# The last pass of a two-layer convolution kernel: channels in chunks of 32 on the partitions, 32x32 transposes on VectorE, layer norm over four partition blocks

## The chip, the cores and the metric

The kernel runs on one core of one Trainium2 chip. A core has TensorE (PE; its weight loads are listed as PEld), VectorE (DVE), ScalarE (ACT), GpSimd (POOL) and SyncE (SP), which here only issues DMAs; 16 DMA engines serve all queues. Tiles lie in SBUF with 128 partitions; TensorE writes PSUM, which has eight banks of 512 float32 per partition. The metric is the device time of one execution in microseconds (us). All data are float32.

## The reference

The input `x` is 8 images of 96 x 96 pixels with 192 channels. Two layers follow, each `x = x + layer(group_norm(x))`. Cut to its shape:

```python
# layer 0
proj  = gn(x) @ W_in + b_in                    # 192 -> 384 channels
local = depthwise_conv3x3(proj)
mixed = 0.25 * (four one-sided moving averages of local) + local
x     = x + (layer_norm(mixed) * ln_g + ln_b) @ W_out + b_out

# layer 1
y = depthwise_conv7x7(gn(x), dw_kernel) + dw_bias
mu  = mean(y, axis=-1); var = mean((y - mu)**2, axis=-1)     # over the 192 channels
y = (y - mu) * rsqrt(var + 1e-6) * ln_gamma + ln_beta
y = gelu(y @ w0 + b0)                          # 192 -> 768
y = y @ w1 + b1                                # 768 -> 192
x = x + y * gamma
```

## The kernel before

The program has five stages, one after the other in one instruction stream for each engine, with the order written out by hand (`tc.manual_schedule`). Each engine works through its own instructions in order; semaphores tie the engines together. The first two stages (to about 1808 us) are the projection, the 3x3 convolution and the moving averages of layer 0; they are not touched.

The third stage (to about 2645 us) has 192 units `u`: it loads `mt` and `xr`, multiplies by `wc` (L989), normalises, adds and stores `X1_d`, the input of layer 1. At its start `load_weights` (L728) issues on ScalarE's queue all loads of the weights of the last pass: `w0w` (w0, rows on partitions in three column blocks), `aff` (the layer norm's gamma and beta, one value per partition), `w1g`, biases. Near its end, at `u == n_u - 20`, it loads the first data of the depthwise convolution: `load_band(0)` and three `load_raw(0, t)`.

The fourth stage is the 7x7 depthwise convolution. It works on 32 items `n`, each 12 channels of one half of the batch. `load_raw(n, t)` (L774) brings a third `t` of the input; one half goes through SP's queue, the other through GpSimd's. `scale_steps(n)` (L804) are 24 VectorE scalings `raw` to `xin` (L820) and one copy of `band` (L824). `conv_d(n, c)` (L1126) is 24 matmuls (L1141) into two PSUM banks and two ScalarE copies to `yo`; `store_d(n)` writes `Y_d`. `N1` = 19 items run here. `raw` has three buffers in each of two pools, one of which (`early`) stays for the whole rest of the program.

The fifth stage, the last pass, begins at about 3002 us. It has 72 units `u`, two for each of 36 blocks `n`. A unit is eight image columns by 128 rows. For each block, `load_y(n)` (L1179) reads the convolution's result with four DMAs into `y`, with image rows on the partitions and 192 channels by 16 columns along them; `load_r(n)` reads the residual and `bias_r(n)` (L1200) adds the bias on GpSimd. For each unit:

- `stats_e` (L1204): for each of eight columns a mean and variance over 192 channels (L1209, L1210), then `rsqrt_eps`: an addition on VectorE (L28) and a power on GpSimd (L29).
- `norm_e` (L1215): eight subtract-and-multiply operations (L1219) from `y` to `yn`.
- `turn_in(u, k)` for k = 0, 1, 2 (L1228): four TensorE transposes each (L1236) into the one PSUM bank of `ps_t`, and a VectorE copy of 512 elements to `yT` (L1239), which also turns the order of the rows round. Now channels are on the partitions: block 0 holds channels 0 to 127 of even columns, block 2 channels 64 to 191 of odd columns, and block 1 the remaining 64 of both.
- `first_layer` (L1244): matmuls L1254 over 128 rows and L1264 over 64 rows into PSUM banks `hp`, then Gelu on ScalarE (L1273) into `g`.
- `second_layer(u, k)` for k = 0 to 3 (L1277): matmuls L1284 into one bank, on VectorE the sum with the residual (L1295) to `xo`, and a GpSimd-issued store of the output (L1303).

In iteration `u` of the loop (L1374) the first layer of `u`, the turning of `u + 1`, the statistics and normalisation of `u + 2` and the second layer of `u - 1` are interleaved. In the first half the first layer is split into three parts and only the banks of `ps_h` (five) are used; the remaining 13 items of the convolution are spread over it by `slot()`, five slots per unit from `u` = 2 on, nine slots per item (three of scalings, six of `conv_d`, which uses the two banks of `ps_y`). In the second half the first layer has two parts and takes its banks from both pools in turn. Before the loop stand `prepare(0)` (run beside the last item of stage four), `load_y(0)`, `load_y(1)`, `turn_in(0, k)`, `prepare(1)` and `load_y(2)`. `load_y(m)` is issued at the end of a unit, once `norm_e` has read the buffer that it fills.

## Time and profile before

| | |
|---|---|
| median of three runs | 5611.91 us (5606.21 to 5626.06) |
| the profiled execution: its own time, its span | 5613.02 us, 5611.2 us |
| mean granted TensorE clock | 0.981 |
| busy: PE, DVE, ACT, POOL | 5384.6, 3068.6, 2241.1, 2099.1 us |
| PEld | 3433.2 us |
| L1236, transposes on TensorE | 864, busy 141.2 us, 285 ns each |
| L1239, their copies on VectorE | 216, 689 ns each |
| L1209, L1210, statistics | 576 each, 460 and 182 ns |
| L1219, normalisation | 576, 445 ns |
| L1295, residual sum | 288, 800 ns |
| L1200, bias on GpSimd | 36, 5440 ns |
| DMA moved | 996.64 MB |

A group is named by line, engine, operation, what it writes and what it reads. Busy time is the union of a group's instructions, so that overlapping matmuls are not counted twice; the mean is of one instruction. Idle time before a group names what ended the wait. A float32 matmul appears as two instructions where it multiplies (24 for L1254 per unit), a transpose as one. Of the span, the last pass is the part after about 3002 us.

### The profile page before, as it was taken

The page shows a single profiled execution, that of the slowest core. Times are in us where ns is not written, and L with a number is a line of the kernel's source. Part 1 is how long each engine was busy: PE and PEld are TensorE (multiplying, and loading weights), DVE is VectorE, ACT ScalarE, POOL GpSimd, SP SyncE. Part 2 cuts the span into 40 slices and gives each one's busy share as a digit, 9 for nine tenths or more (in the row PEclk, how much of TensorE's full clock was granted, in tenths as well). Part 3 has the DMA queues.
Part 4 walks back from the last instruction along what each step waited for, and adds up shares of the span by engine and source line. Part 5 has one row for each costly group of instructions (what it writes and reads, how often), then busy time and mean ns, then how long its engine had stood idle before and what let it go on. Part 6 is the DMA issues. An engine that isn't in the chain of part 4 may idle for free.

```text
span 5611.2 us, 106882 instructions
## 1 busy us (share of the span) xinstructions
PE 5384.6 (96%) x43070; PEld 3433.2 (61%) x43070; DVE 3068.6 (55%) x6331; ACT 2241.1 (40%) x5306; POOL 2099.1 (37%) x2086
## 2 busy tenths in 40 slices
PE   5999989999999999998777999999999999999999
PEld 3666643333333899997344666666666676767677
DVE  5555549999999355555454454444444343333332
ACT  2444447777776566565332222222222222222221
POOL 1111128888888455554222222222222222222221
PEclk9999989999999999999888999999999999999999
DMA  7999869999998899999997456555332223332321
GB/s 199 284 286 278 236 195 245 245 245 243 244 245 214 250 283 283 280 289 275 266 275 173 107 119 133 122 130 116 96 75 69 70 68 78 71 71 68 75 63 40
DMA packets 698886, 996.64 MB, mean 178 GB/s; under 512 B 237415, under 2 KB 579992, under 8 KB 696344
## 3 DMA queue, kind: packets, MB, share of 16 engines
q1 hardware_dynamic: 602200, 622.03, 44.8%
q0 software_dynamic: 90064, 365.17, 20.8%
q8 instruction: 340, 5.57, 0.4%
q10 hardware_dynamic: 6128, 2.61, 0.2%
q14 instruction: 154, 1.26, 0.1%
HBM read 585.22 MB, written 419.95 MB: 179 GB/s over the span
## 4 chain that ended last, share of the span: by engine, by line
PE 45%; DMA 4%; issue 2%; DVE 1%; POOL 0%; SPq 0%; ACT 0%; POOLq 0%; DVEq 0%; ACTq 0%
PE hp L1284 19%; PE hp L1254 13%; PE hp L1264 7%; PE hp L1141 4%; PE pt L1236 2%; DMA raw<-X 2%; DMA band<-Z_d 2%; DVE xin L820 1%; DMA r<-X 0%; DVE band L824 0%; DMA Y<-yo 0%; ACT xin L818 0%; POOL out_dram L1303 0%; SPq L789 0%; POOL r L1200 0%
## 5 line engine op out<-in xcount | busy, mean ns | idle before, releaser
L1284 PE MATMUL hp<-w1g,g 128*128 128x192 f32 x6912 | 1168.6, 328 | 3.4 <-DVE xo L1295 3.2
L1273 ACT ACTIVATE g<-hp,b0g 128x512 f32<-128x512 f32 x864 | 519.0, 691 | 1627.6 <-PE hp L1264 1627.6
L1284 PEld LDWEIGHTS hp<-w1g,g 128*128 128x128 f32 x6912 | 1123.1, 191 | 40.3 <-issue 19.3
L1303 POOL DMA_DIRECT2D out_dram<-xo x288 | 211.6, 735 | 1617.7 <-DVE xo L1295 1575.9
L1254 PE MATMUL hp<-yT,w0w 128*128 128x512 f32 x1728 | 778.4, 597 | 0.0
L989 PE MATMUL po<-wc,mt 128*128 128x193 f32 x3456 | 685.1, 334 | 1.8 <-DVE x1c L1006 1.8
L1239 DVE COPY yT<-pt 128x512 f32<-128x512 f32 x216 | 148.9, 689 | 926.9 <-PE pt L1236 926.8
L600 PE MATMUL pl<-pin,band 34*32 34x380 f32 (+1 forms) x13824 | 628.3, 489 | 18.7 <-DMA pin<-P_d 18.7
L674 POOL TENSOR_TENSOR mo<-mo,z 128x768 f32<-128x768 f32 x286 | 598.6, 2093 | 2.9
L989 PEld LDWEIGHTS po<-wc,mt 128*128 128x128 f32 x3456 | 554.9, 191 | 32.5 <-ACT mean L991 30.3
L1254 PEld LDWEIGHTS hp<-yT,w0w 128*128 128x128 f32 x1728 | 319.7, 190 | 356.8 <-issue 347.2
L633 DVE TENSOR_TENSOR_SCAN z<-decay,loc 128x768 f32<-128x768 f32 x288 | 505.7, 1756 | 41.4 <-ACT loc L609 12.2
L1295 DVE TENSOR_TENSOR xo<-hp,r 128x384 f32<-128x384 f32 x288 | 230.5, 800 | 524.6 <-PE hp L1284 524.6
L1141 PE MATMUL hp<-xin,band 63*64 63x372 f32 (+1 forms) x4608 | 428.5, 511 | 77.0 <-DMA band<-Z_d 38.2
L642 DVE TENSOR_TENSOR_SCAN z<-decay,z 128x768 f32<-128x768 f32 x288 | 498.2, 1730 | 0.1
L600 PEld LDWEIGHTS pl<-pin,band 34*32 34x32 f32 x13824 | 232.2, 107 | 396.5 <-issue 394.6
L621 PE MATMUL pa<-loc,mix 128*32 128x384 f32 x3456 | 431.6, 493 | 0.0
L1151 ACT ACTIVATE yo<-hp,dwb 128x384 f32<-128x384 f32 x384 | 201.6, 577 | 567.6 <-PE hp L1141 440.7
L624 PE MATMUL pa<-last,down 96*32 96x384 f32 x1152 | 426.6, 493 | 0.9 <-ACT mo L625 0.9
L1264 PE MATMUL hp<-yT,w0w 64*128 64x512 f32 x1728 | 419.6, 611 | 0.0
L382 PE MATMUL pm<-xT,win 128*128 128x384 f32 x1152 | 395.1, 493 | 8.1 <-DVE po L406 8.1
L609 ACT COPY loc<-pl 128x384 f32<-128x384 f32 x576 | 248.1, 483 | 311.0 <-PE pl L600 311.0
(143 smaller groups left out, 6636.3 us busy)
## 6 DMA issues: line engine op xcount, KB each, us to landing
P_d<-po POOLq DMA_DIRECT2D x96, 1152.0 KB, 9.8
pin<-P_d SPq DMA_DIRECT2D x192, 576.0 KB
mt<-M SPq DMA_DIRECT2D x192, 384.0 KB
xq<-in_x_dram SPq DMA_DIRECT2D x96, 576.0 KB
xr<-in_x_dram SPq DMA_DIRECT2D x192, 288.0 KB
X<-x1c SPq DMA_DIRECT2D x144, 384.0 KB
y<-Y SPq DMA_DIRECT2D x144, 384.0 KB
r<-X SPq DMA_DIRECT2D x36, 1536.0 KB
```

What stands on the lines that cost most here:

```text
L600: nc.tensor.matmul(pls[g][at * RB : (at + 1) * RB, :, lo:hi], band[rows, c, kh, :], pin[rows, c, :, NJ - 1 - j, lo + kh - 1 : hi + kh - 1] ...
L621: nc.tensor.matmul(pa[at], mix[:, i, at], loc[:, q], start=True, stop=True)
L624: nc.tensor.matmul(pa[at], down[:, to], last[:, q], start=True, stop=True)
L633: nc.vector.tensor_tensor_scan(zf, decay_f, loc.rearrange("p q n -> p (q n)"), 0.0, ALU.mult, ALU.add)
L642: nc.vector.tensor_tensor_scan(zr, decay_f, zr, 0.0, ALU.mult, ALU.add)
L674: eng.tensor_tensor(m, m, z, ALU.add)
L989: nc.tensor.matmul(po, lhs[m], wc[:, m], start=(m == 0), stop=(m == NC - 1))
L1141: nc.tensor.matmul(pys[g][k * 64 : (k + 1) * 64, :, lo:hi], band[rows, k * GS + c, d * ZS : d * ZS + 64], xin[rows, :, :, k * GS + c, lo + ...
L1254: nc.tensor.matmul(hps[m, q], w0w[:, 2 * q, m * 128 : (m + 1) * 128], yT[:, 2 * q], start=True, stop=False,)
L1264: nc.tensor.matmul(hps[m, q], w0w[p, 1, m * 128 : (m + 1) * 128], yT[p, 1], start=False, stop=True,)
L1273: nc.scalar.activation(g[:, m, q], hps[m, q], AF.Gelu, bias=b0g[:, m : m + 1], scale=1.0)
L1284: nc.tensor.matmul(po[:, q], g[:, m, q, k * 128 : (k + 1) * 128], w1g[:, m], start=(m == 0), stop=(m == NE - 1),)
```

## The change

`y` is read in another layout. The 192 channels are cut into six chunks of 32. Four chunks lie on the four partition blocks of 32 in tile `ya`; chunks 4 and 5 lie in tile `yb`, each twice: once for the first four columns of a unit and once, shifted by `HV` = 4 columns, for the last four. Within a partition block the 32 partitions are the image rows. The convolution stores groups of six channels, so a chunk is five whole groups and two channels of a later group; the rows of `w0` and of the layer norm's gamma and beta are loaded in the same permuted order. `load_y` becomes 40 DMAs.

A 32x32 transpose of each block on VectorE then puts 32 channels on each block's partitions. TensorE's transposes, their PSUM bank and the copies from PSUM are gone, and `ps_h` has six banks. As the channels of one pixel now lie on several partition blocks, the layer norm becomes six steps, given out over the unit: `sums` (over the 32 channels of each block), `mean` (gather the blocks' sums by short copies onto 32 partitions, add them, copy the mean back to four blocks), `center` (subtract; Square on ScalarE), `squares` (add), `powers` (gather again, power on GpSimd over 32 partitions by 32 columns), `scale` (copy to four blocks, multiply).

A second-layer step now takes columns `v` and `v + 4` in place of `v` and `v + 1`. `load_y(n + 2)` is issued in the first unit of block `n`, after the turning of the block's second unit. `raw` now has two buffers in `early` and four in the other pool; the third `t = 2` is loaded after the first scalings of its own item, and parts of the loads move to earlier slots. `load_weights` returns 54 loads that are issued one per unit of the third stage from `u` = 8.

The diff, cut to its core:

```diff
-    w0w = cp.tile([128, 3, EXP], F32, name="w0w")
+    w0w = cp.tile([128, 2, EXP], F32, name="w0w")
...
     def load_raw(n, t):
         hf, i = todo[n]
-        pool = d_pools[0 if n == 0 or n >= N1 else (n + 1) % 2]
-        raw = pool.tile([128, NH, NV, GC, WQ], F32, tag="raw", name="raw", bufs=NT)
+        own = 0 < n < N1 and (n % 2 == 0 or t == NT - 1)
+        raw = d_pools[own].tile(
+            [128, NH, NV, GC, WQ], F32, tag="raw", name="raw", bufs=4 if own else 2
+        )
...
-            load_weights()
+            weights = load_weights()
             for u in range(n_u + 1):
+                if weights and u >= 8:
+                    with nc.allow_non_contiguous_dma(reason="one value per partition"):
+                        nc.scalar.dma_start(*weights.pop(0))
...
                 if u == n_u - 20:
                     load_band(0)
-                    for t in range(NT):
+                    for t in range(NT - 1):
                         load_raw(0, t)
                     first_d += scale_steps(0)
-                if u >= n_u - 10:
+                    for k, (n, t) in enumerate(((0, 2), (1, 0), (1, 1))):
+                        first_d.insert(
+                            (k + 1) * 8 + k, lambda n=n, t=t: load_raw(n, t)
+                        )
+                if u >= n_u - 14:
...
-    ps_t = ctx.enter_context(tc.tile_pool(name="e_ps_t", bufs=1, space=PSUM, **by_tile))
-    ps_h = ctx.enter_context(tc.tile_pool(name="e_ps_h", bufs=5, space=PSUM, **by_tile))
+    ps_h = ctx.enter_context(tc.tile_pool(name="e_ps_h", bufs=6, space=PSUM, **by_tile))
...
     def load_y(n):
         hf, p, a, j = place(n)
-        ys[n] = ip.tile([128, D, WQ], F32, tag="y", name=f"y_{n}")
-        r = (NJ3 - 1 - j) * PH + PH - 1 - p
-        q = S // NJ3
-        for b in range(NH):
+        ya[n] = ip.tile([128, NH, CK, WQ], F32, tag="ya", name=f"ya_{n}")
+        yb[n] = ip.tile([128, NH * CK * WQ + HV], F32, tag="yb", name=f"yb_{n}")
+        y = Y_d[hf][(NJ3 - 1 - j) * PH + PH - 1 - p :: NJ3 * PH]
+        main = CK // GS
+        for q in range(8):
...
+            for b in range(NH):
+                nc.sync.dma_start(
+                    dst[:, b, : main * GS * WQ].rearrange("i (g n) -> i g n", g=main),
+                    y[:, chunk * main : (chunk + 1) * main, b, a],
+                )
...
             nc.sync.dma_start(
-                ys[n][b * q : (b + 1) * q].rearrange("h (g c) v -> h g (c v)", c=GS),
-                Y_d[hf][r :: NJ3 * PH, :, b, a],
+                dst[:, :, main * GS * WQ :],
+                y[:, g, :, a, c * WQ : (c + CK - main * GS) * WQ],
             )
...
+    def norm_steps_e(u):
...
+        def gather(name):
+            s, T = t_["s"], sp.tile([CK, 6, NH, WE], F32, tag="T", name="T", bufs=2)
+            for q in range(4):
+                nc.vector.tensor_copy(T[:, q], s[q * CK : (q + 1) * CK, :, :WE])
+            for q in range(4):
+                nc.vector.tensor_copy(
+                    T[:, 4 + q % 2, :, q // 2 * HV : (q // 2 + 1) * HV],
+                    s[q * CK : (q + 1) * CK, :, WE:],
+                )
+            t_[name] = tot = sp.tile([CK, NH, WE], F32, tag=name, name=name, bufs=2)
+            nc.vector.tensor_reduce(tot, T.rearrange("i k b v -> i b v k"), AX.X, ALU.add)
+
+        def spread(name):
+            tot = t_[name]
+            t_["m"] = m = sp.tile([128, NH, WE + HV], F32, tag="m", name="m", bufs=2)
+            for q in range(4):
+                p = slice(q * CK, (q + 1) * CK)
+                nc.vector.tensor_copy(m[p, :, :WE], tot)
+                nc.vector.tensor_copy(
+                    m[p, :, WE:], tot[:, :, q // 2 * HV : (q // 2 + 1) * HV]
+                )
+
+        def apply(op):
+            m = t_["m"]
+            for y, w in both():
+                nc.vector.tensor_tensor(
+                    y, y, m[:, :, w].unsqueeze(2).to_broadcast(list(y.shape)), op
+                )
+
+        def sums():
+            t_["s"] = s = sp.tile([128, NH, WE + HV], F32, tag="s", name="s", bufs=2)
+            for y, w in both():
+                nc.vector.tensor_reduce(
+                    s[:, :, w], y.rearrange("p b c v -> p b v c"), AX.X, ALU.add
+                )
...
+        return [sums, mean, center, squares, powers, scale]
...
-        for n in range(NP):
-            nc.tensor.transpose(pt[:, n], yp[:, n, k * 128 : (k + 1) * 128], ident)
-
-        q = S // NJ3
-        nc.vector.tensor_copy(
-            yTs[u][:, k].rearrange("p n (b h) -> p (n b) h", h=q),
-            pt.rearrange("p n (b h) -> p (n b) h", h=q)[:, :, ::-1],
+        at = t * WE + (HV if k == 2 else 0)
+        y = view_b(n) if k == 1 else ya[n]
+        nc.vector.transpose(
+            yTs[u][:, k, :, :, ::-1],
+            y[:, :, :, at : at + HV].rearrange("p b c v -> p v b c"),
         )
...
-            slots += [scales[:8], scales[8:16], scales[16:]]
+            per_t = len(scales) // NT
+            slots += [scales[:per_t], scales[per_t : 2 * per_t], scales[2 * per_t :]]
+            slots[-3].append(lambda n=n: load_raw(n, NT - 1))
+            if more:
+                for t in range(NT - 1):
+                    slots[t - 2].append(lambda n=n, t=t: load_raw(n + 1, t))
...
             first_layer(u, 0, parts, pool)
-            turn_in(u + 1, 0) if u < n_u else None
+            turn_in(u + 1, 0)
+            turn_in(u + 1, 2)
+            turn_in(u + 1, 1)
+            if t == 0 and n + 2 < n_y and u < n_u:
...
+                load_y(n + 2)
             slot()
```

In the rest of the loop `next(norms)()` stands after the first residual load and then before or after each second-layer step, so that the six steps of unit `u + 2` are given out over unit `u` in their order; `powers` comes after the third second-layer step, `scale` at the unit's end.

## The prediction

> **What bounds the kernel now.** I read the page's slices first, for which engine is full where, then busy time by windows over the last pass, then TensorE in order of time inside one of its units, then the groups kept apart by shape, and last GpSimd beside VectorE. The windows, with busy time of PE, PEld, DVE, ACT and POOL, then the granted clock, DMA share and GB/s:
>
> ```profile
> 2660.00:3000.00 340.00, 257.18 (x2683) 139.39 (x2687) 165.32 (x478) 122.72 (x237) 83.91 (x116) 0.84 0.99 266
> 3100.00:4040.00 940.00, 934.55 (x5386) 588.13 (x5388) 423.39 (x1035) 245.57 (x426) 215.21 (x203) 1.00 0.53 118
> 4040.00:5600.00 1560.00, 1560.00 (x7357) 1099.86 (x7350) 598.55 (x1443) 336.04 (x562) 337.66 (x261) 1.00 0.29 69
> ```
>
> Three regimes. Before about 3000 us the depthwise convolution is bound by DMA (0.99). From 3002 us on the last pass is bound by TensorE: without a gap in its second part, nearly so in the first, where the rest of the convolution is mixed in. VectorE is at 45% and 38% there. The chain of waits names TensorE lines from 3046 us to the end.
>
> TensorE in order of time (start, length, line):
>
> ```profile
> 4514.39 0.60 PE L1236 MATMUL pt<-ident,yn 128*128 128x128 f32 x4
> 4514.83 5.32 PE L1254 MATMUL hp<-yT,w0w 128*128 128x512 f32 x12
> 4520.07 2.85 PE L1264 MATMUL hp<-yT,w0w 64*128 64x512 f32 x12
> 4522.85 0.65 PE L1236 MATMUL pt<-ident,yn 128*128 128x128 f32 x4
> 4523.34 7.97 PE L1284 MATMUL hp<-w1g,g 128*128 128x192 f32 x48
> ```
>
> The transposes (L1236) stand in line with the matmuls. From start to start they occupy 0.44 us in the first place, 0.49 in the second, and a unit has a third group of 0.49: 1.42 us. A unit repeats every 33.07 us (L1254 starts at 4531.15 and again at 4564.22).
>
> The rows that price the new VectorE and GpSimd work:
>
> ```profile
> L866 DVE TENSOR_TENSOR gn_d<-gn_d 128x384 f32<-128x384 f32 x2 | 1.1, 558 | 0.1
> L756 DVE TENSOR_TENSOR w1g<-w1g,lsc 128x192 f32<-128x192 f32 x6 | 1.7, 349 | 0.0
> L871 DVE TENSOR_REDUCE gn_ds<-gn_d 128x32 f32<-128x384 f32 x2 | 1.1, 554 | 0.1
> L79 DVE TENSOR_REDUCE gn_ds<-gn_d 96x32 f32<-96x256 f32 x8 | 3.3, 416 | 0.0
> L444 DVE COPY mix<-down 32x32 f32<-32x32 f32 x27 | 3.1, 167 | 0.1
> L880 POOL TENSOR_TENSOR gn_rb<-gn_ve,neg_half 128x32 f32<-128x32 f32 x2 | 11.0, 5476 | 0.0
> ```
>
> Two-input operations and reductions both cost 1.09 ns per element and 0.14 us; a 32x32 copy between partition blocks 0.167 us; a power over 32 columns 5.48 us (over 8 columns, L29, 1.66).
>
> GpSimd can hold VectorE up:
>
> ```profile
> 3305.70 6.73 DVE L820 TENSOR_SCALAR xin<-raw,s 128x192 f32<-128x192 f32 x3
> ```
> ```profile
> 3306.86 5.44 POOL L1200 TENSOR_TENSOR r<-r,b1g 128x3072 f32<-128x3072 f32 x1
> ```
>
> Three scalings whose median is 0.37 us each took 6.73 us while L1200 ran, and TensorE then waited 3.16 us for L1295 at 3317.79.
>
> **What the Trainium skill says.** VectorE: DVE Perf Modes, "The three transpose paths": VectorE transposes 32x32 blocks only, within SBUF; that is why the layout must change. No row of before shows it. Vector Engine (DVE) Microarchitecture Reference, "3.8 The reshape front-end and per-opcode configuration": one element per cycle per lane. SBUF — State Buffer, "SBUF: two separate sides": the port pair of VectorE and GpSimd is an exclusive lock; L820 beside L1200 agrees. ScalarE: Activation LUTs, "Table sets: the hidden batching unit": cheap functions lie in every table set; Square is not in its short list. The trace has Square (L993) beside copies with no table load, but never beside Gelu.
>
> **The change, part by part.** *TensorE.* The 12 transposes of each of 72 units go: 72 x 1.42 = 102.2 us, all on the path. Nothing replaces them there; L1254, L1264 and L1284 keep their shapes and counts. The period should become 31.65 us.
>
> *VectorE, per unit.* Gone: three copies L1239 (0.69), eight L1209 and L1210 pairs (about 0.59 from start to start), L28 (0.17), the L1219 group (2.95): 9.9 us. New: three transposes of 512 elements. No row shows one: below, 512 cycles at the 0.96 GHz of VectorE: DVE Perf Modes, "Specifications", 0.53 us (an estimate) plus the fixed 0.14; above, 0.95, from L1209 against L1023 (192 elements at a step of 16 in 454 ns, 288 contiguous in 446, so some 0.5 ns per element more). I take 0.8: 2.4 us. Sums, 1024 and 512 elements at that same step: 1.94 to 2.8, I take 2.4. Mean: 16 short copies 2.67, a reduction of 192 0.35, one small operation 0.17: 3.2. Centre: 1.26 + 0.70 = 1.96. Squares: 1.8. Powers: 8 copies, reduction, scaling 1.9. Scale: 8 copies and 1.96: 3.3. Together 17 us, so VectorE rises from 13.1 to 20.2 us per unit with the unchanged L1295 (4 x 0.80). In the second part that is 64% of 31.65: hidden by TensorE. Square on ScalarE costs 1.84 us (0.89 ns per element from L1273 against L1151), hidden as ACT is at 22%; were each unit to reload tables twice, 2 x 1.28 us on ACT would be hidden too.
>
> *Waits in the second part.* The power (5.48 us) is issued some 2.7 us after second-layer step 2 ends; scale waits for it, then come three transposes and the sums, so L1295 of the next step 0 is up to 2 us late. Its bank is wanted 12 us after its matmuls: no stall. The PSUM bank freed from the transposes adds to that slack. Cost 0.
>
> *First part (units to about 26).* Those units took 40.9 us and have on average 0.55 of the 10.4 us of scalings and band copy: VectorE 20.2 + 5.8 = 26 of 39.5 us, with ACT and GpSimd waits about 30. But it works in order. Between steps 1 and 2 of the second layer TensorE spends 3.9 us, while VectorE may have to do 8 scalings (3.0), centre (2.0), wait for Square (1.9), squares (1.8), and in one unit of two sit behind L1200 (5.4). L1295 is then 5.6 to 11 us late against 9.4 us until its bank is reused (six banks instead of five). Some 13 places with about 0.5 us each: 6 us. Further, the last third of each `raw` is loaded only two slots (some 13 us) before it is used; it landed in 4.8 to 14 us (median 7.0) in this part, but three or four times it falls behind the 40 transfers of `load_y` on SP, which at the 0.38 us of short SP issues hold that queue some 15 us. Three waits of 2 us after slack: 6 us. Together 12 us; bounds 0 and 70.
>
> *Start of the pass.* `prepare(0)` ran 2987.69 to 2997.4, beside the last convolution (to 3001.7). The six steps with their two engine changes take about 22 us, so the first layer starts near 3011 instead of 3005, and the second call delays unit 1. Against it stand 12 us that before lost at 3036 to 3047 behind L1200. I take +5, bounds -8 and +20.
>
> *Loads.* `load_y` moves a third more bytes (two chunks twice): 0.5 MB more per load, 6144 pieces instead of 4096 of 384 bytes. In the second part DMA goes from 0.29 to perhaps 0.38: hidden. Two loads fall in the DMA-bound stage: 1.05 MB at 266 GB/s is 4 us, with the short pieces +6; bounds 0 and 20 (SP held with other loads behind). The moved `raw` loads bring no bytes; they move 1.57 MB from a full stage into the end of the block before, also near full: 0.
>
> *Weights.* Some 20 issues on ACT at 1807 to 1825 us, just where TensorE waits (7.5 us busy in 1810 to 1840), become 54 spread over units of that block. DMA was at 0.77 in that hole, so not all of it is theirs: -6, bounds 0 and -20.
>
> Sum against the profiled execution's own time, 5613.0 (span 5611.2 and 1.8 around it): 5613 - 102 + 12 + 5 + 6 - 6 = 5528; the median of the runs is 1.1 lower, so 5527.
>
> **The rivals.** *Smaller gain:* the late scalings and waits eat 50 us more in the first part; the L820 row beside L1200 speaks for it, the six banks against it: 5577. *Slower:* VectorE becomes the bound, at the short copies. For: 32 per unit, each dependent on a small neighbour. Against: L444. With d us for all 32, the first 26 units need 30 - 5.3 + d against 39.5, the last 46 need 15 + d against 31.65. It decides from d = 17.3 (0.54 us a copy), where 26 x 2.5 + 46 x 0.65 = 95 us are lost, nearly all of the gain; at 0.65 us each it loses 26 x 6 + 46 x 4.2 = 349 and gives 5876. A transpose split into its 16 blocks (16 x 0.167 = 2.7 us) would add 5.6 us per unit and not decide it alone. *The change does less than said:* the transposes' TensorE time was overlap, not place; the start-to-start gaps speak against it: 5600.
>
> **How the numbers follow.** Forecast 0.66, smaller gain 0.19, slower 0.11, nothing moved 0.04. Least: 5527 with all loads and weights at their good ends (start -13, loads -6, weights -14, first part -12) is 5482; I take 5488, as not all come together. Top: the smaller gain with a worse start, 5585; what is left out is about 0.19. A measurement of this kernel tells 0.3% (17 us) from no change: faster 0.85, same 0.04, slower 0.11.
>
> **What would show it.** Right: L1236 gone, a period near 31.6 us after 4000 us, no VectorE line ahead of idle TensorE there, VectorE near 20 us per unit. Wrong: short copies over 0.3 us, TensorE in the first part waiting for L1295's successor, `raw` waits on VectorE inside the last pass, or a later start than 3015 us.

## The result: slower, by the queue that the loads share

The changed kernel takes 5707.35 us, the median of four runs (5690.05 to 5711.55), against 5615.03 us for the kernel before in the same sessions: a ratio of 1.0158, with a 95% interval from 1.0129 to 1.0186. It is 92 us slower; the prediction was 5527 us, in a range that ended at 5585. The profiled execution took 5710.79 us, its span is 5708.9 us.

The windows of the changed kernel at places like those shown of before (columns as there: busy time of PE, PEld, DVE, ACT and POOL, then the granted clock, DMA share and GB/s):

```profile
2660.00:3000.00 340.00, 243.98 (x2550) 142.44 (x2542) 151.30 (x435) 117.38 (x226) 83.78 (x116) 0.84 0.94 251
3100.00:4040.00 940.00, 822.64 (x4504) 506.57 (x4503) 551.52 (x1312) 272.93 (x415) 274.57 (x182) 0.93 0.47 112
4200.00:5600.00 1400.00, 1400.00 (x6314) 968.94 (x6313) 998.74 (x2178) 438.43 (x617) 485.08 (x241) 1.00 0.31 82
```

The last row is what the change set out to do: TensorE has no gap, and VectorE is at 71%. The middle row is the loss: in the part of the last pass where the rest of the convolution is mixed in, TensorE was busy for 934.55 of 940 us before and is now busy for 822.64. VectorE is at 59% there; whether its work is on the path, a share does not tell, the experiments do.

One unit of the second part on TensorE, in order of time (start, length, line):

```profile
4810.11 5.31 PE L1353 MATMUL hp<-yT,w0w 128*128 128x512 f32 x12
4815.35 2.85 PE L1363 MATMUL hp<-yT,w0w 64*128 64x512 f32 x12
4818.13 8.07 PE L1383 MATMUL hp<-w1g,g 128*128 128x192 f32 x48
4826.03 5.31 PE L1353 MATMUL hp<-yT,w0w 128*128 128x512 f32 x12
...
4841.96 5.31 PE L1353 MATMUL hp<-yT,w0w 128*128 128x512 f32 x12
```

The transposes are gone, and the unit repeats after 31.85 us (4810.11 to 4841.96) where it took 33.07. The 48 second-layer matmuls hold their place for 7.90 us (4818.13 to 4826.03) where they held 7.80 before (4804.22 to 4812.02 in the trace of before); that is 0.1 us twice per unit, and so 1.22 us are won instead of 1.42.

Cut at three events, the profiled executions compare as follows. The first column runs from the convolution's first matmul to the first matmul of the last pass's first layer, the second from there to the convolution's last matmul, the third from there to the end. What lies before is left out: the convolution began between 2638.8 and 2657.2 us in the fourteen traces of this study, so that up to 18 us between two single times can come from the early stages.

| us | convolution alone | last pass, first part | second part | sum |
|---|---|---|---|---|
| before | 357.8 | 1035.1 | 1571.1 | 2964.0 |
| after | 399.1 | 1144.6 | 1515.2 | 3058.9 |

The second part won 55.9 us. The convolution's stage lost 41.3 and the first part 109.5. Where TensorE stood, two places of the changed kernel's timeline show. The first is the end of the convolution's stage (SPq is SP's DMA queue; the bracket holds the engine's idle time before the row and what ended it):

```profile
2957.68 11.63 SPq L1220 DMA_DIRECT2D ya<-Y  x4
...
2978.75 0.30 SPq L1226 DMA_DIRECT2D ya<-Y  x1
...
3002.43 1.87 SPq L1220 DMA_DIRECT2D yb<-Y  x4
3006.03 0.30 SPq L1226 DMA_DIRECT2D yb<-Y  x1
3006.37 1.87 SPq L1220 DMA_DIRECT2D yb<-Y  x4
3009.82 0.30 SPq L1226 DMA_DIRECT2D yb<-Y  x1
3010.22 1.92 SPq L807 DMA_DIRECT2D raw<-X  x3
...
3013.78 2.39 SPq L817 DMA_DIRECT2D band<-Z_d  x1
3014.84 7.04 DVE L838 TENSOR_SCALAR xin<-raw,s 128x192 f32<-128x192 f32 x24 [35.50 <-DMA raw<-X]
...
3023.85 16.45 PE L1167 MATMUL hp<-xin,band 63*64 63x384 f32 x144 [30.93 <-DMA band<-Z_d]
```

One call of `load_y` holds SP's queue from 2957.68 to 3010.1 us. Behind it stand the last `raw`, the stores of `Y` and the `band` of the last item; TensorE stands 30.93 us until that `band` is in. In `ya` a short piece (L1226) mostly follows its four long ones at once; the one at 2978.75 waited 9.3 us for a store of `Y`. In `yb` each comes some 1.6 us or more after them, because it waits for them: the two copies overlap in memory, and it is probably taken for a second write to the same place (read from the code; no run tried it). The list of waits gives `SPq L1226 <- DMA yb<-Y: 273.0, 161, 9.3` (us in total, times, longest).

The second place is one of the regular ones, inside the last pass:

```profile
3849.53 1.76 SPq L1220 DMA_DIRECT2D ya<-Y  x4
...
3882.09 0.30 SPq L1226 DMA_DIRECT2D yb<-Y  x1
3882.44 0.44 SPq L1193 DMA_DIRECT2D Y<-yo  x1
...
3885.97 1.69 SPq L817 DMA_DIRECT2D band<-Z_d  x1
3887.77 11.39 SPq L807 DMA_DIRECT2D raw<-X  x3
3896.14 2.41 DVE L838 TENSOR_SCALAR xin<-raw,s 128x192 f32<-128x192 f32 x8 [20.10 <-DMA raw<-X]
3898.32 1.54 PE L1167 MATMUL hp<-xin,band 63*64 63x384 f32 x2 [18.68 <-DVE xin L838]
```

Here a call holds the queue for 32.9 us. The other calls of this part hold it for 26 to 36 us; only the first two of all, at 2957.68 and 3020.28, hold it for 52.4 and 42.8. In the kernel before, such a load (an earlier one) is one row:

```profile
3323.05 3.78 SPq L1185 DMA_DIRECT2D y<-Y  x4
```

The waits from 3000 to 4200 us close the chain: VectorE's wait for `raw`, which the kernel before does not have there, counts 134.2 us in eight places. One of them, 35.5 us, is the one shown at the end of the convolution's stage; the other seven, 98.7 us, lie in the last pass. VectorE copies `band` (L842) after the scalings, so that TensorE's waits for that copy are in the main the same delay, one step on.

```profile
DVE xin L838 <- DMA raw<-X: 134.2, 8, 35.5
PE hp L1167 <- DVE band L842: 88.3, 9, 26.3
PE hp L1167 <- DMA band<-Z_d: 30.9, 1, 30.9
PE hp L1353 <- ACT g L1372: 18.0, 2, 14.7
```

### The profile page after: what moved, and what is told of

Same layout as the page of the kernel before. It is cut to its first block, busy times and chain, and to the rows that moved or that the text cites. A ratio compares the mean times of both kernels' runs of the same rounds, so it can differ in the third digit from the quotient of the medians.

```text
span 5708.9 us, 108585 instructions
## 1 busy us (share of the span) xinstructions
PE 5328.3 (93%) x42206; PEld 3359.1 (59%) x42206; DVE 3725.5 (65%) x7626; ACT 2442.2 (43%) x5450; POOL 2377.0 (42%) x2086
## 3 DMA queue, kind: packets, MB, share of 16 engines
q0 software_dynamic: 90064, 365.17, 20.4%
## 4 chain that ended last, share of the span: by engine, by line
PE 38%; DMA 6%; DVE 4%; issue 3%; SPq 1%; POOL 1%; ACT 0%; DVEq 0%; POOLq 0%; ACTq 0%
PE hp L1383 17%; PE hp L1353 11%; PE hp L1363 6%; PE hp L1167 4%; DMA raw<-X 3%; DMA band<-Z_d 2%; DVE xin L838 1%; POOL rs L1317 1%; SPq L1220 1%; DMA yb<-Y 1%; DVE yb L1284 1%; DMA ya<-Y 0%; DVE band L842 0%; DVE ya L1284 0%; DVE xo L1394 0%
## 5 line engine op out<-in xcount | busy, mean ns | idle before, releaser
L1167 PE MATMUL hp<-xin,band 63*64 63x372 f32 (+1 forms) x4608 | 448.7, 525 | 233.4 <-DVE band L842 106.0
L600 PE MATMUL pl<-pin,band 34*32 34x380 f32 (+1 forms) x13824 | 638.6, 495 | 18.8 <-DMA pin<-P_d 18.6
L1167 PEld LDWEIGHTS hp<-xin,band 63*64 63x64 f32 x4608 | 218.5, 145 | 432.9 <-issue 253.1
L1317 POOL TENSOR_TENSOR rs<-var,neg_half 32x32 f32<-32x32 f32 x72 | 392.2, 5447 | 158.9 <-DVE var L1315 158.8
```

The lines of the kernel that those rows point to most:

```text
L600: nc.tensor.matmul(pls[g][at * RB : (at + 1) * RB, :, lo:hi], band[rows, c, kh, :], pin[rows, c, :, NJ - 1 - j, lo + kh - 1 : hi + kh - 1] ...
L1167: nc.tensor.matmul(pys[g][k * 64 : (k + 1) * 64, :, lo:hi], band[rows, k * GS + c, d * ZS : d * ZS + 64], xin[rows, :, :, k * GS + c, lo + ...
L1317: nc.gpsimd.tensor_tensor(rs.rearrange("i b v -> i (b v)"), var.rearrange("i b v -> i (b v)"), neg_half[:CK, : NH * WE], ALU.pow,)
```

## The experiments

Three theories stood at the start. T1: the 40 DMAs of `load_y`, with the waits among them, hold SP's queue, and `raw`, `band` and the stores of `Y` behind them are late; the short lead of the new `raw` loads (the time between the place of a load in the order and its use) makes it harmful. T2: VectorE, which works in order, has too much to do. T3: more and shorter pieces make the transfers slow. The kernel before took 5621.67 us beside the first four runs, 5618.46 beside the next four, and 5614.37 and 5619.10 (medians) beside the two last pairs. The first eight runs were timed once each; small differences among them are read from the stretches in the table at the end of this section.

**Another queue for what stands behind the loads.**

```diff
-        for g, eng in enumerate((nc.sync, nc.gpsimd)):
+        engs = (nc.gpsimd, nc.gpsimd) if n >= N1 - 1 else (nc.sync, nc.gpsimd)
+        for g, eng in enumerate(engs):
...
-        (nc.sync, nc.gpsimd)[g].dma_start(
+        (nc.gpsimd if n >= N1 - 1 else nc.sync, nc.gpsimd)[g].dma_start(
             band[g * 64 : (g + 1) * 64].rearrange("q c l -> q (c l)"),
```

> From item 18 of the convolution on, both halves of every raw load and every band load are issued on GpSimd's queue, so none stands behind load_y on SP; everything else is as in the changed kernel. Theory 1 (load_y's 40 DMAs hold SP's queue, and raw and band behind them come late): the DVE waits for raw in the last pass fall from 80 us to under 20, the 31 us gap of TensorE before the last item of stage four goes, time 5600 (5570 to 5640). Theory 2 (VectorE has too much to do in order in the first part): raw waits may fall but others take their place, 5690 to 5715. Theory 3 (a third more bytes in more and shorter pieces slow all transfers): 5690 to 5715, since the bytes are the same.

5622.22 us: 85 us less than the changed kernel's median, as T1 wants, though 22 above its figure. `load_y` and its transfers are as in the changed kernel, so T3 cannot explain the loss by itself. VectorE's wait for `raw` fell from 134.2 to 2.2 us. What remained shows other things behind the same queue. One is the stores of `Y`:

```profile
3835.46 0.30 SPq L1227 DMA_DIRECT2D yb<-Y  x1
3835.80 0.44 SPq L1194 DMA_DIRECT2D Y<-yo  x1
...
3844.13 4.38 PE L1168 MATMUL hp<-xin,band 63*64 63x384 f32 x24 [12.92 <-ACT yo L1178]
```

The eviction to `yo` waited 22.75 us, to 3843.49, for the store of an earlier `yo`, whose half on SP's queue was issued only at 3835.80, right behind the last piece of `load_y`. The other is `load_y` itself: at 3026.90 TensorE had stood 20.36 us for an eviction that was queued on ScalarE behind the first Square of the norm. That Square started at 3023.69, when VectorE had centred `ya`; VectorE had waited 13.24 us for the last of `yb`, to 3018.28.

**The short pieces last, so that nothing waits inside the group of 40.**

```diff
+        rest = []
         for q in range(8):
...
-            nc.sync.dma_start(
-                dst[:, :, main * GS * WQ :],
-                y[:, g, :, a, c * WQ : (c + CK - main * GS) * WQ],
-            )
+            rest.append(
+                (
+                    dst[:, :, main * GS * WQ :],
+                    y[:, g, :, a, c * WQ : (c + CK - main * GS) * WQ],
+                )
+            )
+        for dst, src in rest:
+            nc.sync.dma_start(dst, src)
```

> In load_y the eight short DMAs of the last two channels of each chunk are issued after all 32 long ones, instead of one after every four. Theory 1: SP waits before each short DMA of yb for the four before it (some 3.5 us each, 273 us in all); with this order a load holds SP for about 20 us instead of 33, raw comes earlier, time 5660 (5630 to 5685). Theories 2 and 3: no change, 5690 to 5715.

5655.8 us, as expected: the calls in the last pass's first part hold the queue for 19 to 30 us instead of 26 to 36 (the first call, in the convolution's stage, still for 46.7, from 2942.05 to 2988.8), VectorE's wait for `raw` is 67.3 us instead of 134.2, and about half of the loss is back.

**The norm left out.** `norm_steps_e` returns six steps that do nothing, so the layer norm of layer 1 is not computed.

> The six steps of the layer norm in the last pass are left out, so the first layer works on y as loaded; transposes, loads and all else stay. VectorE has 17 us less per unit, ScalarE and GpSimd lose Square and the power. Theory 2: the loss of the first part goes with it, time at or under 5540. Theory 1: the raw waits and the hold of SP stay, and only the start of the pass (some 35 us of gaps between 3040 and 3110) gets shorter: 5640 to 5690. Theory 3: as theory 1.

5648.81 us. With nearly all of VectorE's new work gone, its wait for `raw` in that stretch is still 138.7 us in 11 places, and TensorE's wait for `band` 32.9. T2 falls as the cause of those waits. The 58 us that went show that the norm costs something in the kernel whose queue is held; the run does not say how much of it would stay with a free queue.

**The lead of `raw` as before.** Three buffers in each pool and the old load times; the edit undoes that part of the change.

```diff
-        own = 0 < n < N1 and (n % 2 == 0 or t == NT - 1)
-        raw = d_pools[own].tile(
-            [128, NH, NV, GC, WQ], F32, tag="raw", name="raw", bufs=4 if own else 2
-        )
+        pool = d_pools[0 if n == 0 or n >= N1 else (n + 1) % 2]
+        raw = pool.tile([128, NH, NV, GC, WQ], F32, tag="raw", name="raw", bufs=NT)
...
-            slots[-3].append(lambda n=n: load_raw(n, NT - 1))
-            if more:
-                for t in range(NT - 1):
-                    slots[t - 2].append(lambda n=n, t=t: load_raw(n + 1, t))
             slots += [[lambda n=n, c=c: conv_d(n, c, ps_y)] for c in range(GS)]
+            if more:
+                slots[-GS] += [lambda n=n, t=t: load_raw(n + 1, t) for t in range(NT)]
```

> The raw loads are put back as in the kernel before: three buffers in each pool, all three thirds loaded in the first convolution slot of the item before, 48 us ahead of use instead of two slots; load_y is unchanged. Theory 1 in the form that the short lead is what makes SP's hold hurt: raw waits in the last pass under 10 us, the first part recovers 70 to 100 us, stage four keeps its loss, 5600 to 5640. Theory 1 with the hold alone (33 us or more against any lead): 5660 to 5690. Theories 2 and 3: 5690 to 5715.

5595.3 us, 5 below the range given for T1. In the first part no wait for `raw` is left; the calls of `load_y` are much as they were (25 to 43 us), but the data are there before they are needed; one hole of 11.71 us for `band` is new there. The stage ahead won 20.4 us, most of it in its first item (see "Why the prediction was wrong"), though its hole for `band`, which has no lead there, stayed:

```profile
3005.83 11.82 PE L1161 MATMUL hp<-xin,band 63*64 63x384 f32 x96 [35.56 <-DMA band<-Z_d]
```

**`load_y` taken apart, the lead of `raw` short.** The function returns ten groups of four DMAs (the short pieces last), and two groups are issued at each slot.

```diff
         def slot():
             if slots and u >= 2:
                 for step in slots.pop(0):
                     step()
+            issue(parts_y[:2])
+            del parts_y[:2]
...
-                load_y(n + 2)
+                parts_y += load_y(n + 2)
```

> The changed kernel with load_y's issues taken apart: eight groups of four DMAs and then the eight short pieces in two groups of four, two groups at each of the five places of a unit instead of all 40 in one piece; and in the convolution's stage load_y(0) and load_y(1) stand behind the raw loads of their item instead of ahead of them. The short raw lead of the change stays. T1 (40 DMAs in one piece hold SP's queue): the queue is held 4 us at a time, the short lead does little harm, 5565 us, 5540 to 5595, and the wait of VectorE's xin for raw falls under 40 us of its 193. If the short lead does harm by itself: 5620 to 5670 with waits for raw over 100 us. T2 or T3 (VectorE too busy, or the pieces' transfers themselves): no better than the 5655.8 of the run with the last pieces last.

5607.43 us, between the ranges of T1 and of a harmful lead: the wait for `raw` fell to 18.6 us, so the short lead by itself does little harm. (Ahead of a load SP also waits until VectorE has turned the old data out of the buffer: 222.1 us in 13 places between 3000 and 4200 us in the changed kernel. This run still has 186.4 us of it in eight places, so it is not what made the waits for `raw`.) In the convolution's stage `load_y(0)` now stood behind its item's `raw`, but still in front of the next `band`, and a hole of 25.5 us for `band` remained.

**Both together**, `load_y` taken apart and `raw` as before.

> As the run before it, and the raw buffers and their load times as before the change. T1: the 5595.3 of the run with raw as before loses the hole of 35 us at the end of the convolution's stage and the few us of later waits: 5550 us, 5530 to 5570. If it is the raw lead alone that counts and SP's queue not: 5590 to 5600. If with the queue free the lead is worth nothing: the same as the run before it to 10 us.

5579.59 us, 10 above the range: VectorE and TensorE have no wait for `raw` or `band` left in the stretch from 3000 us on, the hole for `band` just ahead of it is still there (23.48 us), and the start of the last pass has gaps of its own. The longest of them:

```profile
3062.45 1.96 ACT L1310 ACTIVATE sq<-ya 128x1024 f32<-128x1024 f32 x1 [18.81 <-DMA r<-X]
...
3065.08 2.38 ACT L1378 ACTIVATE g<-hp,b0g 128x512 f32<-128x512 f32 x4
...
3065.79 3.78 PE L1359 MATMUL hp<-yT,w0w 128*128 128x512 f32 x4 [15.76 <-ACT g L1378]
```

A Square of unit 2 stands on ScalarE ahead of the Gelus of unit 1, and ScalarE works in order. The Square can start only when VectorE has centred its data, here at 3062.4, because the `y` of that unit landed at about 3055. The name in the first bracket is only what came last by the profile; the data come from VectorE's L1290.

**The squares of unit 1 emitted later.**

```diff
-        for step in norm_steps_e(1):
-            step()
         bias_r(0)
...
             first_layer(u, 0, parts, pool)
+            if u == 0:
+                for step in norm_steps_e(1):
+                    step()
```

> As the run before it, and the norm steps of unit 1 are emitted behind the first third of unit 0's first layer instead of ahead of it, so that no Square that waits for VectorE stands on ScalarE ahead of the first Gelus. If ScalarE's order is what opens the hole of 14.7 us at the start of the last pass: 10 to 15 us less than the run before it, so about 5537. If the hole is the normalisation's own chain on VectorE: the same to 4 us, with the hole at another place within the first two units.

5595.57 us, a miss: 16 more than the run before it, 14.0 of them from the convolution on. The order on ScalarE was mended, but on GpSimd `bias_r(0)`, which waits for `r`, now stood in front of unit 1's power, and the load of `r` stood on SP behind `load_y(1)`. VectorE waited 34.5 us for that power, TensorE 35.68 us for `yT`.

**The kernel before, with a `load_y` of many DMAs.** Nothing else of the change is in this run.

```diff
         for b in range(NH):
-            nc.sync.dma_start(
-                ys[n][b * q : (b + 1) * q].rearrange("h (g c) v -> h g (c v)", c=GS),
-                Y_d[hf][r :: NJ3 * PH, :, b, a],
-            )
+            for g in range(0, GROUPS, 2):
+                nc.sync.dma_start(
+                    ys[n][b * q : (b + 1) * q, g * GS : (g + 2) * GS].rearrange(
+                        "h (g c) v -> h g (c v)", c=GS
+                    ),
+                    Y_d[hf][r :: NJ3 * PH, g : g + 2, b, a],
+                )
```

> The kernel before with load_y alone in 32 DMAs of two channel groups in place of 2 DMAs of 32, in one piece, no write-after-write among them; raw lead, norm and transposes as before. T1: a hold of 32 x 0.46 = 15 us a time against a raw lead that is long: 0 to 20 us slower than the kernel before, so 5615 to 5635, and the harm in the changed kernel needs its longer holds (33 to 52 us) or its short lead. If the number of DMAs alone does the harm: 5660 or more. If the shorter pieces slow the transfers of all queues: slower by as much in the late part too, where no raw is loaded.

5672.17 us, 54 more than the kernel before, and by the expectation's words a mark for the number of DMAs alone. Its arithmetic was wrong: the loop runs over four pairs of images, so that a call is 4 x 16 = 64 DMAs and not 32, and one late call holds the queue for 38.53 us, not for 15:

```profile
3861.78 38.53 SPq L1186 DMA_DIRECT2D y<-Y  x64
```

Its calls hold the queue for 31 to 42 us in the first part, somewhat longer than the changed kernel's, with few waits among the pieces. The first call (57.1 us) opened the same hole at the end of the convolution's stage (35.61 us for `band`, 35.56 in the run with `raw` as before), and VectorE's one wait for `raw` (40.0 us, to 3003.0) lies there too. In the first part, with the long lead of the kernel before, no wait for `raw` is left. That part lost 33 us all the same: TensorE has new gaps of 11.04 us at 3061 (VectorE waited 15.43 us for a late `y`), 4.84 (`band`) and 7.58 (an eviction to `yo`), and was busy for some 10 us more. The second part took 1571.1 us, exactly that of before: there such holds cost nothing, as no loads of the convolution stand behind them. T3 is not needed in the last pass: the run with both has all transfers of the changed kernel and no wait for `raw`. In the convolution's stage this run shows that a hold opens the hole without more bytes; what more bytes add there, no run tells.

**The first load on two queues, behind the last `band`.** On the run with both together:

```diff
+                if n == NI + 1:
+                    issue(load_y(0), (nc.sync, nc.gpsimd))
-                    if n == NI:
-                        issue(load_y(0))
...
-            issue(load_y(1))
...
         load_r(0)
+        issue(load_y(1))
```

> The run with raw as before and load_y taken apart (5579.6 us), with two loads placed anew: load_y(0) is issued one item later, behind the Y stores and the band of the convolution's last item but one, in pairs of DMAs that alternate between SP's and GpSimd's queues; load_y(1) stands behind load_r(0). T1: the hole of 23.5 us for band at the end of the convolution's stage goes, and load_y(0) lands after some 17 us of issue on two queues instead of 35 on one, so that the last pass starts at about 3005 us instead of 3022.8, and the end comes at 5555 us, 5540 to 5568. If the transfers and not the issues set when load_y(0) is in: the band's hole goes, but the last pass starts at 3018 or later, and the end is 5570 to 5582.

5577.70 us (five runs, 5571.99 to 5582.12), ratio to before 0.9937, 0.9916 to 0.9959. The hole for `band` went. The start came at 3019.9 us and not at 3005, but this profiled run began its convolution 10.9 us later than the run before it (2657.1, 2646.2). Counted from there the start is 13.8 us earlier (362.8 against 376.6), where 17.8 were expected, and the sums of unit 0 end 13.7 us earlier. So the start is nearly as in the first branch, and only the end is in the range of the second. What it won was lost again in part: a new hole of 12.00 us stands where the convolution's evictions are behind a Square, and the one at unit 1, where `load_y(1)` is later still, grew from 15.76 to 26.66.

**The same, with the squares of unit 1 late**, as in the run that missed, with `r` now ahead of `load_y(1)`.

> As the run before it, with the norm steps of unit 1 emitted behind the first third of unit 0's first layer. In the run where this was tried with load_y(1) ahead of load_r(0), bias_r stood on GpSimd in front of unit 1's powers and waited for r, which stood on SP behind load_y(1): a wait of 34.5 us. If that was the cause of its loss, it is gone here, and the run is between 10 us less than the run before it and equal to it. If the order itself is bad because unit 1's normalisation, 22 us long, then ends after unit 0's first layer: 5 to 15 us more than the run before it.

5579.78 us (seven runs), ratio 0.9938, 0.9918 to 0.9959: equal to the run before it. Unit 1's power now came after 22.6 us instead of 34.5, and a hole of 23.82 us for `yT` took the place of the one for Gelus.

**The second load one item earlier.**

```diff
                 if n == N1 - 1:
+                    issue(load_y(1))
                     for step in norm_steps_e(0):
                         step()
...
         load_r(0)
-        issue(load_y(1))
```

> The run with the first load on two queues (5577.7 us), with load_y(1) issued at the convolution's last item of the first 19, in front of its norm steps, instead of behind load_r(0) at the start of the last pass. In the run before, TensorE stood 26.7 us at unit 1 for Gelus on ScalarE that were queued behind the Square of unit 2, whose y had not landed. If the late y is the cause: that hole falls to under 10 us and the end to 5560 us, 5550 to 5568. If it is ScalarE's order alone, or VectorE's chain of 22 us a unit at the start: the hole keeps 20 us or more at unit 1, and the end stays at 5572 to 5582.

5564.02 us (four runs, 5559.61 to 5570.15), ratio 0.9905, 0.9883 to 0.9926: the best of the study, about 53 us below the kernel before and 143 below the change as it was. The hole at unit 1 shrank from 26.66 to 15.16 us, less than expected. That the time fell into the expected range is mostly luck: the profiled run began its convolution 18 us earlier than the run before it, at the early edge of the spread; from the convolution on it took 2919.0 us against 2923.2, and the two intervals overlap.

**The squares of the first four units on VectorE.**

```diff
-                nc.scalar.activation(to, y, AF.Square)
+                if u < 4:
+                    nc.vector.tensor_tensor(to, y, y, ALU.mult)
+                else:
+                    nc.scalar.activation(to, y, AF.Square)
```

> As the run before it, and the squares of units 0 to 3 are made by VectorE (a product of y with itself) instead of by ScalarE, so that nothing that waits for the normalisation stands on ScalarE ahead of Gelus and of the convolution's evictions there. If ScalarE's order costs the holes (12.0 us before the convolution's last matmuls of that stage, 4.2 and what is left at unit 1): 5545 us, 5535 to 5555, and the last pass starts at 3015 or earlier. If VectorE's own chain is what is late: equal to the run before it to 5 us.

5571.31 us (four runs, 5561.51 to 5581.90), ratio 0.9911, 0.9882 to 0.9941, whose interval overlaps that of the run before it almost wholly. From the convolution on the two profiled runs took 2922.9 and 2919.0 us. The three holes for ScalarE are gone, and these are in their place (TensorE, same columns as above):

```profile
3028.70 6.38 PE L1361 MATMUL hp<-yT,w0w 128*128 128x512 f32 x8 [26.06 <-DVE yT L1346]
3054.34 5.44 PE L1361 MATMUL hp<-yT,w0w 128*128 128x512 f32 x8 [6.25 <-DVE yT L1346]
3089.06 5.62 PE L1391 MATMUL hp<-w1g,g 128*128 128x192 f32 x24 [13.81 <-DVE xo L1402]
```

So ScalarE's order only hid what lies ahead of it. In this run VectorE waits 9.32 us for `y` and starts the sums at 3000.22, waits 4.22 us more ahead of the sums over `yb` and 5.56 us for the power, and reaches the first transpose at 3027.53. At the start of the pass the bound is the landing of the load and the normalisation's chain behind it; no run parts the two.

The experiments' profiled executions, cut as the two above:

| us | convolution alone | first part | second part | sum |
|---|---|---|---|---|
| `raw`, `band` on GpSimd | 385.1 | 1066.0 | 1514.2 | 2965.3 |
| short pieces last | 385.6 | 1110.8 | 1515.3 | 3011.7 |
| no norm | 381.4 | 1098.7 | 1515.3 | 2995.4 |
| `raw` as before | 378.7 | 1047.1 | 1515.3 | 2941.1 |
| `load_y` taken apart | 382.8 | 1060.1 | 1515.3 | 2958.2 |
| both | 376.6 | 1039.7 | 1515.3 | 2931.6 |
| both, late squares | 368.6 | 1061.7 | 1515.3 | 2945.6 |
| before, 64 DMAs | 379.1 | 1068.1 | 1571.1 | 3018.3 |
| first load on two queues | 362.8 | 1047.5 | 1512.9 | 2923.2 |
| and late squares | 364.8 | 1048.9 | 1512.9 | 2926.6 |
| second load early | 368.9 | 1037.2 | 1512.9 | 2919.0 |
| and squares on VectorE | 371.5 | 1038.5 | 1512.9 | 2922.9 |

## Why the prediction was wrong

*The step that failed* is the one for the first part: "three or four times it falls behind the 40 transfers of `load_y` on SP, which at the 0.38 us of short SP issues hold that queue some 15 us", priced at "Three waits of 2 us after slack: 6 us" inside 12 us with bounds 0 and 70. The mechanism was named, its size was not. The four issues of a group take 1.8 us, 0.46 each, so that forty are some 18 us; in `yb` a fifth waits for its four predecessors, and some issues take longer. A call of the first part holds the queue for 26 to 36 us instead of 15 (the first two for 52.4 and 42.8), and seven waits of VectorE for `raw`, 5.3 to 25.5 us each, stand in place of three of 2 us. The first part should have become 1035.1 - 26 x 1.42 + 12 = 1010 us and took 1144.6. Only `raw` was followed past the hold, though `band` and the stores of `Y` go through the same queue. Undoing the lead alone brought the first part to 1047.1, taking the loads apart alone to 1060.1, both to 1039.7: either of the two edits would have kept most of it, and they do not add up, as each takes away the other's harm. The 64 DMAs in the kernel before show the hold alone with the long lead: 33 us in that part. Two of the forecast's signs of being wrong came: waits for `raw` inside the last pass, and a start after 3015 us (3049.1).

*Loads in the convolution's stage*: +6 with bounds 0 and 20 "(SP held with other loads behind)", and *start of the pass*: +5. Together that stage was to lose 11 us and lost 41.3. Three places make 38 of them: the hole for `band` at its end (30.93 us, where before has 14.21), 8.84 us ahead of the first matmul of the first layer, and the hole at its first item, 19.71 us where before has 7.32. The row of before for the first, and the rows of the changed kernel for the last:

```profile
2986.25 15.48 PE L1141 MATMUL hp<-xin,band 63*64 63x384 f32 x144 [14.21 <-DMA band<-Z_d]
```
```profile
2676.97 3.61 ACT L836 ACTIVATE xin<-raw,s 128x192 f32<-128x192 f32 x8 [16.25 <-DMA raw<-X]
2681.10 18.15 PE L1167 MATMUL hp<-xin,band 63*64 63x384 f32 x192 [19.71 <-ACT yo L1177]
```

This last hole belongs to a term that the forecast put at 0, the moved `raw` loads. The last third of item 1's `raw` now stands on SP's queue behind the last stores of `X` and was issued at 2669.75; its scalings on ScalarE waited for it with the evictions to `yo` behind them. The hole is 17.57 to 19.71 us in the five versions with the moved loads and 5.16 to 5.40 in the seven with `raw` as before. The bytes of `load_y` came as counted (18.7 MB more in all). The kernel before with 64 DMAs lost 21.3 us in that stage by the hold. The best version still loses 11.1 us there; that this is the forecast's sum is chance, as its loads are placed otherwise.

*Bounds.* The upper bound of 70 us stood for late scalings and waits of a few us. A queue's hold was in none of the rivals, and so the whole range lay below the time that came. The slower rival named the direction, but by another mechanism: short copies that decide from 0.54 us each. They take 0.16 to 0.22 us, and VectorE needs 998.74 / 1400 x 31.85 = 22.7 us per unit, near the 20.2 of the forecast.

*Second part.* Right in kind, and 14% less in size: 1.22 us per unit for 1.42, because the second layer's matmuls hold their place 0.1 us longer twice. No VectorE line stands ahead of an idle TensorE there.

*Single prices* (the changed kernel's groups; after the bar busy time and the mean in ns, then idle time before):

```profile
L1338 DVE STREAM_TRANSPOSE yT<-ya 128x512 f32<-128x512 f32 x144 | 143.1, 1031 | 0.0
L1262 DVE COPY T<-s 32x32 f32<-32x32 f32 x576 | 98.3, 171 | 6.1
L1284 DVE TENSOR_TENSOR yb<-yb,m 128x512 f32<-128x512 f32 x144 | 258.0, 1791 | 0.0
L1304 ACT ACTIVATE sq<-ya 128x1024 f32<-128x1024 f32 x72 | 144.0, 2001 | 575.2 <-issue 289.5 <-DVE ya L1284 285.7
```

A transpose takes 1.03 us, above the upper bound of 0.95, and 0.36 above the lower estimate of 0.67 (0.53 + 0.14) from the clock in the Trainium skill's VectorE: DVE Perf Modes, "Specifications"; the measurement decides. The operation on `yb` takes 0.68 us when alone; its mean is 1.79 because some take up to 6.02 us beside GpSimd's sum on `r`, as L820 did before. The Squares take 2.00 + 1.10 us instead of 1.84 in total; they were called hidden "as ACT is at 22%". A share does not say that: at the start of the pass the Square waits for VectorE with Gelus behind it, and TensorE stood 14.71 us for these.

*Weights.* The forecast was -6. From the second stage's last scan to the first matmul with `wc` it was 32.0 us before (1805.5 to 1837.5) and is 22.0 (1820.3 to 1842.3), so 10 us were won in the hole itself, and as much in every run that has this part of the change. The stages ahead of it ended 15 us later in this trace; in the other traces that have the change they end between 1810.1 and 1829.4 us, and no run tells how much of this is spread.

*What stays open.* From the convolution on, the best version is 45.0 us below before (2964.0 to 2919.0); by the forecast's own terms it should have been 102 - 12 - 5 - 6 = 79. Of the 34 that are missing, 27 are in the first part (1037.2 against 1010), seven in the second. In the first part TensorE's gaps at its start (4.14 and 15.16 us) are part of it; by the run with squares on VectorE the landing of the load and the norm's chain are behind these. Small gaps ahead of the convolution's matmuls, where VectorE's copy of `band` is late, make up more: 20.7 us in seven places, where before has 2.1. No run was made on these.

## What to carry to other kernels

When a load is cut into many DMAs, count the issues and the waits among them, and follow everything that stands behind them on the same queue: the price is the time for which the queue is held, less the lead of what is behind. The changed kernel's loads hold the queue for some 26 us each in the second part and harm nothing there; ahead of the last `band` of the convolution's stage a hold of 52 us ended in a hole of 31, though neither the bytes nor any engine's busy time show it. Issue it in groups between the loads that have little lead, and before shortening a lead look at what else was added to that queue.

## What the runs showed that was not expected

A matmul group after a gap runs slowly: 24 matmuls of the convolution took 2.13 us when TensorE had been busy (3850.61 in the changed kernel) and 4.04 us after a gap of 13.50 us:

```profile
3486.24 4.04 PE L1167 MATMUL hp<-xin,band 63*64 63x384 f32 x24 [13.50 <-DVE band L842]
```

so that a gap costs more than its own length. In the best version, after a gap of 6.34 us (3112.96), it was the same 4.04. The granted clock was 0.50 in both of these stretches and 1.00 in that of the 2.13 us.

Square and Gelu alternate on ScalarE through the whole last pass with one load of the activation table, 1.28 us, at the pass's first Gelu; the two reloads per unit that the prediction kept as a possibility did not come. Square is not in the short list that the Trainium skill gives in ScalarE: Activation LUTs, "Table sets: the hidden batching unit"; here it behaves like the functions that are.
